# A halo row copied from the chunk above, and x loaded a chunk one step sooner, in a fused attention and deformable convolution kernel

## The chip, the cores and the metric

The kernel runs on one core of a Trainium2 chip. The metric is the device time of one launch in microseconds (us). The kernel before was timed in three runs: 5197.73 us median, from 5185.96 to 5206.68.

## The reference

The input is eight images of 256 channels and 64 x 64 positions, in float32. Two residual layers are applied:

```
x = x + L0(gn(x))
x = x + L1(gn(x))

gn: subtract the mean and divide by the deviation of each group of 8 channels over an image
L0: q, k, v = 1x1 convolutions; attention of each position over its 3x3 neighbours, 4 heads,
    plus a 3x3 kernel generated from q, k, v for every position; 1x1 projection
L1: om = conv3x3(x)                        27 channels: 9 offset pairs and 9 masks
    sample x bilinearly at 9 moved points (4 corners each), times sigmoid(mask)
    conv 3x3 of the samples, 256 -> 256 channels
```

## The kernel before

The kernel treats the images one after another. An image is cut into 8 chunks of 8 rows (512 positions); 256 channels lie as two halves of 128 partitions.

Each image has three stages. **Attention** (`attention`, L555) works through the 8 chunks, adds the result of layer 0 to the image, which stays in on-chip memory in the one tile `image`, and stores a copy of each finished chunk in DRAM. **Preparation** (`prepare`, L624) works through the 8 chunks again. In its step c it computes the sampling positions and corner weights of chunk c-1 (`positions`, L668: some 13 small VectorE instructions), writes chunk c to a table in DRAM from which the samples will be gathered (`to_table`, L630: transposes on TensorE, three ScalarE copies into the tiles `ts`, six DMAs), convolves chunk c to offsets and masks (`offsets`, L649: 18 matmuls, each recorded as two, and the ScalarE activation L665), takes the statistics of chunk c-1 of the next image (`first_stats`, L257), norms chunk c+1 of this image (`normed`, L220), and at last loads chunk c of the next image over the old chunk c (`load_chunk`, L89). **Sampling and convolution** then runs in 72 slots per image (8 chunks by 9 kernel points): in each slot four gathers by GpSimd (L771), four ScalarE scalings (L787), twelve VectorE multiply-adds (L795), eight TensorE transposes (L816), two ScalarE copies (L819) and four matmuls (L833, each recorded as two).

The slots of image b run together with the attention and the preparation of image b+1, called the front: the main loop (L876) issues one slot and then as many steps of the front as are due, 73 steps in 72 slots with a lead of six. Eight preparations are run in all. The first has no slots beside it; the last has no further image to load. The six between them do both.

The order on TensorE, ScalarE, VectorE and GpSimd is the order in which the program issues its instructions. SyncE, which issues the plain DMAs (loads of x, table writes, the chunk `r` of the kept image read back at L826, the output at L845), is ordered by a scheduler. In the built program the DMAs of one preparation stand on SyncE in this order, where xc is the load of chunk c and tc are the six table writes of chunk c: x0 t0 t1 x1 t2 x2 t3 x3 t4 x4 t5 x5 t6 x6 x7 t7. In the overlapped preparations the output DMA and the read of `r` stand inside and behind t6.

A chunk needs a row above and a row below it for the 3x3 convolution. So `normed` makes 10 rows out of `image` (9 at the first and the last chunk) into one of two tiles `xn`, of 10 rows each. For chunk c+1 it reads the last row of chunk c, and this is why the load over chunk c stands behind it. The positions of one chunk, the table transposes and the offsets of the next share a ring of four PSUM tiles (`ps_a`), so a later `offsets` can only begin when `positions` has read its tile at L689.

Of the kernel before, what the change touches and what calls it, by code (L numbers as in the profile page):

```python
# [9 lines left out]
F32 = mybir.dt.float32  # L10
I32 = mybir.dt.int32
AF = mybir.ActivationFunctionType
ALU = mybir.AluOpType
# [4 lines left out]
P = 128  # L18
C = 256
# [4 lines left out]
R = 8  # L24
N = R * W
NB = N // P
NC = H // R
# [8 lines left out]
TP = R * WP // TJ  # L36
# [21 lines left out]
def preact_kernel(ctx: ExitStack, tc: tile.TileContext, a: dict, out: bass.AP):  # L58
# [17 lines left out]
    nc = tc.nc  # L76
# [3 lines left out]
    const = ctx.enter_context(tc.tile_pool(name="const", bufs=1))  # L80
# [8 lines left out]
    def load_chunk(b, c):  # L89
        s = slice(c * N, (c + 1) * N)  # L90
        nc.sync.dma_start(image[:, :, s], sources[b][:, :, s])
# [31 lines left out]
    base = const_tile("base", [P, NC * NB, 2 * KK])  # L123
    eps = const.tile([P, 1], F32, tag="eps", name="eps")
    nc.vector.memset(eps, EPS)

    wts2 = []
    for i in range(2):
# [4 lines left out]
    xn2 = [const.tile([P, NT, R + 2, WP], F32, tag=f"xn{i}", name=f"xn{i}") for i in range(2)]  # L133
# [47 lines left out]
    p2 = ctx.enter_context(tc.tile_pool(name="p2", bufs=2))  # L181
# [6 lines left out]
    def psum_a(name):  # L188
        return ps_a.tile([P, 512], F32, tag="a", name=name)
# [27 lines left out]
            nc.vector.reciprocal(gn[:, 1, :], std)  # L217
            return gn

    def normed(xt, gn, c):  # L220

        xn = xn2[c % 2]
        lo, hi = max(0, R * c - 1), min(H, R * c + R + 1)
        if c == 0:
            nc.vector.memset(xn[:, :, 0, :], 0.0)
        if c == NC - 1:
            nc.vector.memset(xn[:, :, R + 1, :], 0.0)
        o = lo - (R * c - 1)
        for ct in range(NT):
            nc.vector.tensor_scalar(  # L230
                xn[:, ct, o : o + hi - lo, 1 : W + 1],
                xt[:, ct, lo * W : hi * W].rearrange("p (r w) -> p r w", w=W),
                gn[:, 0, ct : ct + 1],
                gn[:, 1, ct : ct + 1],
                ALU.subtract,
                ALU.mult,
            )
        return xn
# [9 lines left out]
    def window(t, ct, k):  # L248
        dy, dx = divmod(k, 3)
        if ct is None:  # L250
            return t[:, :, dy : dy + R, dx : dx + W]
        return t[:, ct, dy : dy + R, dx : dx + W]
# [4 lines left out]
    def first_stats(b, c):  # L257
        if c == 0:
            stats0[b] = p2.tile([P, NT, NC, 6], F32, tag="stats0", name=f"stats0_{b}")
        for ct in range(NT):  # L260
            nc.vector.bn_stats(
                stats0[b][:, ct, c, :], image[:, ct, c * N : (c + 1) * N]
            )
        if c == NC - 1:
            norm0[b] = Norm(stats0[b], f"0_{b}")
# [289 lines left out]
    def attention(b):  # L555
# [5 lines left out]
        yield None  # L561
        gn = gn.ready()
        xn = normed(xt, gn, 0)
        yield None
        d = None
        for c in range(NC):
# [26 lines left out]
            if c + 1 < NC:  # L593
                xn = normed(xt, gn, c + 1)
# [29 lines left out]
    def prepare(b, gn):  # L624


        xt = image
        table = tables[b % 2].rearrange("e (k c) -> e k c", k=2)

        def to_table(c, xn):  # L630
            for i in range(TJ // 2):
                ps = psum_a(f"ptab_{b}_{c}_{i}").rearrange("p (j e) -> p j e", j=2)
                for j in range(2):
                    o = WP + (2 * i + j) * TP
                    for ct in range(NT):
                        nc.tensor.transpose(
                            ps[:TP, j, ct * P : (ct + 1) * P],
                            xn[:, ct].rearrange("p r w -> p (r w)")[:, o : o + TP],
                            ident,
                        )  # L640
                ts = p2.tile([TP, 2, C], F32, tag="ts", name=f"ts_{b}_{c}_{i}", bufs=3)
                nc.scalar.copy(ts, ps[:TP])
                for q in range(2):
                    e = (R * c + 1 - q) * WP + 2 * i * TP
                    nc.sync.dma_start(
                        table[e : e + 2 * TP, q, :].rearrange("(j p) e -> p j e", p=TP), ts
                    )

        def offsets(c, xn):  # L649

            ps = psum_a(f"om_{b}_{c}")
            n = 0
            for k in range(KK):
                for ct in range(NT):
                    g = n % 4
                    nc.tensor.matmul(  # L656
                        ps[32 * g : 32 * g + 32, :],
                        w_off[:, ct, k, :],
                        window(xn, ct, k),
                        start=(n < 4),  # L660
                        stop=(n >= KK * NT - 4),
                    )
                    n += 1
            om = p1.tile([P, N], F32, tag="gs", name=f"om_{b}_{c}")
            nc.scalar.activation(om, ps, AF.Identity, bias=b_off)  # L665
            return om

        def positions(c, om):  # L668
            u = f"{b}_{c}"
            ps = psum_a(f"omt_{u}")  # L670
            for j in range(NB):
                nc.tensor.matmul(
                    ps[:, j * NOM : (j + 1) * NOM],
                    om[:, j * P : (j + 1) * P],
                    stk_om,
                    start=True,
                    stop=True,
                )
            omt = ps[:, : NB * NOM].rearrange("p (b o) -> p b o", o=NOM)
            S = [P, NB, 2 * KK]  # L680

            def small(name, shape=S, dt=F32):
                return p1.tile(shape, dt, tag=name, name=f"{name}_{u}")

            mk = small("mk", [P, NB, KK])
            nc.scalar.activation(mk, omt[:, :, 18:27], AF.Sigmoid)

            pos = small("pos")
            nc.vector.tensor_add(pos, omt[:, :, 0:18], base[:, c * NB : (c + 1) * NB, :])  # L689
            nc.vector.tensor_scalar(pos, pos, -1.0, float(H), ALU.max, ALU.min)  # L690
            pi = small("pi", dt=I32)
            nc.vector.tensor_copy(pi, pos)
            fl = small("fl")
            nc.vector.tensor_copy(fl, pi)
            gt = small("gt")
            nc.vector.tensor_tensor(gt, fl, pos, ALU.is_gt)
            nc.vector.tensor_sub(fl, fl, gt)

            fr = small("fr", [P, NB * KK, 2, 2])
            pos2 = pos.rearrange("p b (k d) -> p (b k) d", d=2)  # L700
            fl2 = fl.rearrange("p b (k d) -> p (b k) d", d=2)
            nc.vector.tensor_sub(fr[:, :, :, 1], pos2, fl2)
            nc.vector.tensor_scalar(fr[:, :, :, 0], fr[:, :, :, 1], -1.0, 1.0, ALU.mult, ALU.add)
            nc.vector.tensor_mul(
                fr[:, :, 0, :],
                fr[:, :, 0, :],
                mk.rearrange("p b k -> p (b k)").unsqueeze(2).to_broadcast([P, NB * KK, 2]),
            )
            idx = wp.tile([P, NB, KK], I32, tag="idx", name=f"idx_{u}")
            wt = wp.tile([P, NB, KK, 4], F32, tag="wt", name=f"wt_{u}")  # L710
            found[b, c] = idx, wt
            nc.vector.tensor_mul(
                wt.rearrange("p b k (x y) -> p (b k) x y", y=2),
                fr[:, :, 0, :].unsqueeze(2).to_broadcast([P, NB * KK, 2, 2]),
                fr[:, :, 1, :].unsqueeze(3).to_broadcast([P, NB * KK, 2, 2]),
            )

            fi = small("fi", [P, NB * KK])
            nc.vector.tensor_scalar(
                fi, fl2[:, :, 0], float(WP * ES), float((WP + 1) * ES), ALU.mult, ALU.add  # L720
            )
            nc.vector.scalar_tensor_tensor(
                idx.rearrange("p b k -> p (b k)"),
                fl2[:, :, 1],
                float(ES),
                fi,
                ALU.mult,
                ALU.add,
            )

        xn = normed(xt, gn, 0)
        om = None
        for c in range(NC):
            if om is not None:
                positions(c - 1, om)
            to_table(c, xn)
            om = offsets(c, xn)
            if b + 1 < B and c > 0:
                first_stats(b + 1, c - 1)
            if c + 1 < NC:  # L740
                xn = normed(xt, gn, c + 1)
            if b + 1 < B:
                load_chunk(b + 1, c)
            yield
        positions(NC - 1, om)
        if b + 1 < B:
            first_stats(b + 1, NC - 1)
        yield
# [225 lines left out]
```

## Time and profile before

| | |
|---|---|
| median of three timed runs | 5197.73 us |
| the profiled execution's own time | 5546.8 us |
| its span, first to last instruction | 5545.0 us |
| TensorE, VectorE, ScalarE, GpSimd busy | 88%, 75%, 43%, 59% of the span |
| TensorE clock granted, mean | 0.939 |
| DRAM traffic | 1280.19 MB read, 137.13 MB written |

The profiled execution is 6.7% longer than the median of the timed ones, so a sum made in its microseconds has to be carried over to the timed runs. A busy TensorE is no TensorE at its peak, since the ends of matmuls are modelled. The waits of an engine are given with the instruction that was released and with what released it.

### The profile page before, as it was taken

What the parts mean: (1) busy time and instruction counts of PE and PEld (TensorE: products, weight loads), DVE (VectorE), ACT (ScalarE), POOL (GpSimd) and SP (SyncE); (2) the same over time, 40 slices, a digit from 0 to 9 for tenths busy, and PEclk for the clock granted to TensorE, in tenths of its full rate; (3) what the DMA queues carried; (4) which work ended last, traced back from release to release, by engine and by line L of the source; (5) the groups of instructions that cost most, each with busy time, mean ns of one, the idle gap of its engine ahead of it and who ended that gap; (6) DMA issues with size and microseconds to landing.
All of it is one profiled execution on the core that took longest, in us unless ns stands there. A gap on an engine that the chain in (4) does not pass through costs nothing. (4 is left out here: it accounts for less than half of the span.)

```text
span 5545.0 us, 79699 instructions
## 1 busy us (share of the span) xinstructions
PE 4874.6 (88%) x26592; PEld 2725.8 (49%) x26592; DVE 4170.6 (75%) x10071; ACT 2368.6 (43%) x5184; POOL 3287.5 (59%) x2310
## 2 busy tenths in 40 slices
PE   7979998899988998899988999989898899887677
PEld 4545554455544554455544555445554555443333
DVE  4567787788877787778878787878777777876666
ACT  2334444444444444444444444444444444443333
POOL 0036565666646666566656666566664666647776
PEclk9989999999999999999999999999999999998878
DMA  2067777777787777877787777877778677787777
GB/s 85 21 236 251 247 249 278 262 256 260 262 311 249 266 262 283 289 247 265 260 284 278 252 268 252 302 260 258 252 256 322 242 260 258 274 300 275 274 278 279
DMA packets 476840, 1422.60 MB, mean 257 GB/s; under 512 B 46910, under 2 KB 114750, under 8 KB 476300
## 3 DMA queue, kind: packets, MB, share of 16 engines
q0 software_dynamic: 331776, 1208.11, 61.9%
q1 hardware_dynamic: 141902, 204.27, 10.2%
q10 hardware_dynamic: 2750, 5.12, 0.3%
q8 instruction: 210, 3.44, 0.2%
q14 instruction: 202, 1.65, 0.1%
HBM read 1280.19 MB, written 137.13 MB: 256 GB/s over the span
## 5 line engine op out<-in xcount | busy, mean ns | idle before, releaser
L771 POOL DMA_INDIRECT g<-table,idx x2304 | 3284.9, 1426 | 2236.2 <-DVE s L795 585.5
L795 DVE SCALAR_TENSOR_TENSOR s<-g,wt,s 128x256 f32<-128x256 f32 x6912 | 2796.0, 478 | 566.5 <-ACT s L787 399.9
L833 PE MATMUL po<-vt,w_conv 128*128 128x512 f32 x4608 | 2187.8, 620 | 63.0 <-DVE r L844 37.4
L833 PEld LDWEIGHTS po<-vt,w_conv 128*128 128x128 f32 x4608 | 880.2, 202 | 965.9 <-issue 923.9
L787 ACT ACTIVATE s<-g,wt 128x256 f32<-128x256 f32 x2304 | 1068.5, 509 | 562.5 <-DMA g<-table,idx 464.7
L816 PE MATMUL pt<-ident,s 128*128 128x128 f32 x4608 | 725.0, 295 | 262.7 <-ACT vt L819 129.9
L816 PEld LDWEIGHTS pt<-ident,s 128*128 128x128 f32 x4608 | 547.4, 149 | 557.9 <-issue 184.4
L819 ACT COPY vt<-pt 128x512 f32<-128x512 f32 x1152 | 614.7, 584 | 423.3 <-PE pt L816 271.9
L281 PE MATMUL psq<-xn,w_qkvT 128*128 128x512 f32 x512 | 291.1, 720 | 113.2 <-DVE wk L488 108.4
L359 DVE TENSOR_TENSOR qk<-qk,near_k 128x400 f32<-128x400 f32 x256 | 129.8, 567 | 306.1 <-PE qk L351 165.2
L656 PE MATMUL om<-xn,w_off 128*32 128x512 f32 x2304 | 291.9, 604 | 7.7 <-DVE pos L689 7.4
L289 ACT COPY q<-psq 128x512 f32<-128x512 f32 x128 | 75.0, 586 | 483.7 <-PE psq L281 436.2
L313 PE MATMUL psk<-xn,w_qkvT 128*128 128x264 f32 (+1 forms) x1088 | 249.3, 382 | 10.9 <-ACT k L326 10.9
L313 PE MATMUL psv<-xn,w_qkvT 128*128 128x264 f32 (+1 forms) x1088 | 258.4, 382 | 0.0
L281 PEld LDWEIGHTS psq<-xn,w_qkvT 128*128 128x128 f32 x512 | 112.1, 229 | 290.6 <-DVE wk L488 161.1
L528 ACT COPY acc<-av 128x512 f32<-128x512 f32 x128 | 74.9, 585 | 414.4 <-PE av L521 320.8
L533 PE MATMUL proj<-acc,w_projT 128*128 128x512 f32 x512 | 239.8, 596 | 3.3 <-ACT s L787 2.7
L313 PEld LDWEIGHTS psv<-xn,w_qkvT 128*128 128x128 f32 x1088 | 199.9, 190 | 83.3 <-issue 46.4
L313 PEld LDWEIGHTS psk<-xn,w_qkvT 128*128 128x128 f32 x1088 | 202.3, 191 | 73.3 <-issue 20.2
L351 PE MATMUL qk<-k,q 64*64 64x100 f32 x4096 | 165.3, 260 | 78.5 <-issue 75.4
L351 PEld LDWEIGHTS qk<-k,q 64*64 64x64 f32 x4096 | 119.4, 136 | 155.0 <-issue 139.0
L335 ACT COPY v<-psv 128x320 f32<-128x320 f32 (+1 forms) x272 | 111.5, 417 | 187.3 <-PE psv L313 171.1
(89 smaller groups left out, 3375.0 us busy)
## 6 DMA issues: line engine op xcount, KB each, us to landing
table<-ts SPq DMA_DIRECT2D x384, 176.0 KB
g<-table,idx POOLq DMA_INDIRECT x2304
x<-in_x_dram SPq DMA_DIRECT2D x64, 512.0 KB
x<-x SPq DMA_DIRECT2D x64, 512.0 KB
r<-x SPq DMA_DIRECT2D x64, 512.0 KB
out_dram<-r SPq DMA_DIRECT2D x64, 512.0 KB
w_conv<-in_w_conv_dram ACTq DMA_DIRECT2D x1, 2304.0 KB
w_qkv<-in_w_qkv_dram ACTq DMA_DIRECT2D x2, 384.0 KB
```

The source lines that it names most:

```text
L281: nc.tensor.matmul(ps, w_qkvT[:, ct, m * P : (m + 1) * P], window(self.xn, ct, 4), start=(ct == 0), stop=(ct == NT - 1),)
L313: nc.tensor.matmul(ps[:, : (hi - lo) * WP], w_qkvT[:, ct, o : o + P], self.xn[:, ct, lo:hi, :], start=(ct == 0), stop=(ct == NT - 1),)
L351: nc.tensor.matmul(both[h][64 * t : 64 * t + 64, n : n + NK], self.qt[r, ct, o * T * T : (o + 1) * T * T], kt[r, ct, :, T * o : T * o + KT ...
L359: nc.vector.tensor_mul(qk[:, 2 * jj : 2 * jj + 2, :, h, :], both[h][:, : 4 * NK].rearrange("p (j c k) -> p j c k", j=2, c=NT), near_k.unsq ...
L533: nc.tensor.matmul(ps, w_projT[:, ct, m * P : (m + 1) * P], self.acc[:, ct].rearrange("p (t y x) -> p y t x", y=T, x=T), start=(ct == 0), ...
L656: nc.tensor.matmul(ps[32 * g : 32 * g + 32, :], w_off[:, ct, k, :], window(xn, ct, k), start=(n < 4), stop=(n >= KK * NT - 4),)
L771: nc.gpsimd.indirect_dma_start(out=g, out_offset=None, in_=tables[b % 2], in_offset=bass.IndirectOffsetOnAxis(ap=found[b, c][0][:, j, k : ...
L787: nc.scalar.activation(s, g[:, 0:C], AF.Copy, scale=w[:, 0:1])
L795: nc.vector.scalar_tensor_tensor(s, g[:, q * C : (q + 1) * C], w[:, q : q + 1], s, ALU.mult, ALU.add)
L816: nc.tensor.transpose(pt[ct][:, j, :], s[:, ct * P : (ct + 1) * P], ident)
L819: nc.scalar.copy(v[:, ct, :], pt[ct].rearrange("p b n -> p (b n)"))
L833: nc.tensor.matmul(po[:, m, :], w_conv[:, ct, k, m * P : (m + 1) * P], v[:, ct, :], start=(k == 0 and ct == 0), stop=(k == KK - 1 and ct = ...
```

## The change

In the preparation, `normed` is called with `carry=True`. From the second chunk on it then no longer norms the row above the chunk again: it copies this row, for both channel halves in one instruction, from the other `xn` tile, where it was normed as the last row of the chunk above. The copy is a multiplication by a tile that holds 1.0. What `normed` makes out of `image` is 9 rows instead of 10 (8 instead of 9 at the last chunk). The attention calls `normed` as before.

With this, the norming of chunk c+1 reads only chunk c+1 and the first row of chunk c+2. So step c now loads chunk c+1 of the next image instead of chunk c, and step 0 loads chunks 0 and 1. The statistics are taken in the same steps as before. The table tiles `ts` rotate through four buffers instead of three.

On SyncE the order of a preparation becomes x0 t0 x1 t1 x2 t2 x3 t3 x4 t4 x5 t5 x6 t6 x7 t7.

```diff
+    one = const.tile([P, 1], F32, name="one")
+    nc.vector.memset(one, 1.0)
...
-    def normed(xt, gn, c):
+    def normed(xt, gn, c, carry=False):
         xn = xn2[c % 2]
         lo, hi = max(0, R * c - 1), min(H, R * c + R + 1)
+        if carry and c:
+            lo = R * c
+            nc.vector.tensor_scalar(
+                xn[:, :, 0, 1 : W + 1],
+                xn2[(c - 1) % 2][:, :, R, 1 : W + 1],
+                one,
+                None,
+                ALU.mult,
+            )
...
-                ts = p2.tile([TP, 2, C], F32, tag="ts", name=f"ts_{b}_{c}_{i}", bufs=3)
+                ts = p2.tile([TP, 2, C], F32, tag="ts", name=f"ts_{b}_{c}_{i}", bufs=4)
...
             if c + 1 < NC:
-                xn = normed(xt, gn, c + 1)
+                xn = normed(xt, gn, c + 1, carry=True)
             if b + 1 < B:
-                load_chunk(b + 1, c)
+                if c == 0:
+                    load_chunk(b + 1, 0)
+                if c + 1 < NC:
+                    load_chunk(b + 1, c + 1)
             yield
```

## The prediction

> **What bounds the kernel now.** I read the page's busy row, then the waits, then the time line of the preparations, and last the busy time by stretch.
>
> ```profile
> PE 4874.6 (88%) x26592; PEld 2725.8 (49%) x26592; DVE 4170.6 (75%) x10071; ACT 2368.6 (43%) x5184; POOL 3287.5 (59%) x2310
> ...
> DVE stats L261 <- DMA x<-in_x_dram: 72.7, 22, 9.1
> ...
> ACT ts L642 <- DMA table<-ts: 86.7, 48, 5.5
> ```
>
> TensorE has the largest share, 88%. The two waits that the change touches add up to 72.7 us on VectorE (statistics that wait for x; columns: total, times, longest) and 86.7 us on ScalarE (a copy into `ts` that waits until the tile's last table write is done). Shares don't say whether these waits count; for this I look at where they fall. In the stretch from 0 to 60 us L261 waits 7.2 us, for the first loads of the kernel, which stay. The other 65.5 us lie in the six overlapped preparations: 13.6, 10.4, 9.7, 11.9, 9.4 and 10.5 us. In each of them one wait is 8.8 to 9.1 us long, always in step 7. The time line of the second one (start, length, engine, line; in brackets the idle time before and what ended it):
>
> ```profile
> 1614.35 0.40 SPq L91 DMA_DIRECT2D x<-in_x_dram  x1
> ...
> 1631.03 1.08 SPq L91 DMA_DIRECT2D x<-in_x_dram  x2
> ...
> 1639.53 0.58 ACT L642 COPY ts<-ptab 88x512 f32<-88x512 f32 x1 [5.53 <-DMA table<-ts]
> ...
> 1643.65 1.29 DVE L261 BATCH_NORM_STATS2 stats<-x 128x6 f32<-128x512 f32 x2 [9.03 <-DMA x<-in_x_dram]
> ...
> 1647.06 1.09 PE L816 MATMUL pt<-ident,s 128*128 128x128 f32 x4 [5.23 <-DVE s L795]
> 1649.34 1.12 PE L816 MATMUL pt<-ident,s 128*128 128x128 f32 x4 [1.20 <-DVE s L795]
> ```
>
> The loads of chunks 6 and 7 are issued together at 1631.03. VectorE wants chunk 6 at 1634.6 and gets it at 1643.65. The twelve multiply-adds of the running slot stand behind the statistics in VectorE's order, and TensorE's transposes wait for their sums: 5.23 + 1.20 us idle. The other five show 6.11, 6.17, 5.97, 5.64 and 6.18 us. So VectorE's 9 us become 6 on TensorE, with 36.5 us in all six.
>
> Is TensorE what sets the pace there? Two stretches answer, from the first `positions` of a preparation to the last, the second preparation and the eighth, which loads nothing (stretch, length, busy PE, PEld, DVE, ACT, POOL, clock, DMA share, GB/s):
>
> ```profile
> 1564.53:1649.60 85.07, 78.36 (x507) 40.06 (x506) 68.47 (x198) 36.29 (x79) 37.32 (x26) 0.97 0.89 314
> 4865.25:4942.38 77.13, 77.13 (x507) 39.64 (x506) 60.92 (x184) 36.08 (x78) 26.29 (x27) 1.00 0.88 300
> ```
>
> The same 507 TensorE records take 77.13 us without a gap where nothing is loaded, and 85.07 us with 6.7 us of gaps where it is. Between the stalls a step is 11.02 us in both. TensorE sets the pace, and the stall in step 7 is on the path.
>
> **What the Trainium skill says.** "VectorE: DVE Perf Modes", section "Mode 2×_2P — use both read ports for one tensor": float32 from and to on-chip memory runs at two elements per cycle if the outermost dimension is even. The trace agrees in kind: ten rows are faster than nine.
>
> ```profile
> L230 DVE TENSOR_SCALAR xn<-x,gn 128x640 f32<-128x640 f32 x192 | 110.4, 616 | 0.0
> L230 DVE TENSOR_SCALAR xn<-x,gn 128x576 f32<-128x576 f32 x64 | 49.4, 813 | 0.0
> ```
>
> "TensorE: Matmul & The Clock Gate", section "What's actually happening": after an idle window of about 3.4 us the array runs at half clock for a while. The trace agrees: the stretch with the 5.2 us gap has clock 0.97, the one without has 1.00, and from 1646 to 1652 us it is 0.50. "DMA: Bandwidth & Descriptors", section "Queues, rings and completion order": each DMA engine takes the descriptors of one queue in ring order, so a load stands behind the table writes issued before it. This fits the 12.6 us from issue to use of chunk 6; no row here separates it.
>
> **The change part by part.**
>
> *The load a step sooner.* On SyncE chunk 6 is now issued where chunk 5 was, at 1614.35, 20 us before VectorE wants it; the slow loads of step 7 took 12 to 13 us from issue to use. The place has the same condition, the end of `normed`. Chunk 7 stays at about 1631 but alone; its statistics are wanted at 1652.7. All other loads also gain a step; chunk 0 stays, 14 us ahead. The queue between t1 and t6 is as before, each load one chunk ahead; what moves in traffic is one load of 512 KB, from step 7 to step 0. At the 301 GB/s of an early step it is 1.7 us of DMA time, where the share is 0.87 and nothing waits. Gains in the profiled execution:
> - the 36.5 us of TensorE idle in step 7;
> - smaller load waits in mid preparation (3.96 us in the first, 2.05 in the fourth) that hold `positions` and so `offsets` back: TensorE waited 2.12 + 0.64 and 0.64 + 0.84 us there, I take 3 of 4.2;
> - half clock after the gap: eight matmuls L833 took 5.08 us at 992.5 and 3.60 elsewhere. The phase is 6.8 to 10.2 us and costs at most half of that, but TensorE also waits for VectorE in it. Between 0 and 5 us each, I take 2: 12 us.
>
> Sum 51.5 us. The stretches check it: the six last 83.69, 85.07, 84.70, 86.58, 84.45 and 84.34 us against 77.13, which is 46.1 us before the clock.
>
> *The copied row.* Per image VectorE gets seven copies of 128x128 elements. No row shows one; the nearest is the 128x72 form of L690, 224 ns. Below by that, above by 128 elements at one per cycle beside it, some 0.3 us; I take 0.23. Six norms go from ten rows to nine: 2 x (813 - 616) = +0.39 us. With the copy, +0.62 us a step, six times. The seventh goes from nine rows to eight, even again: an estimate from 616 less 128 elements at two per cycle of the 0.96 GHz that the page gives (67 ns) is 0.55, so 2 x (0.55 - 0.81) + 0.23 = -0.3. In all +3.4 us per image, +27 us in eight. The rows taken out cost VectorE more than they save. What hides it: per step VectorE is busy 9.5 to 9.8 of 11.02 us and then idles 0.8 to 1.9 us before L689. Only the step with the output additions is full (13.39 busy in 13.83). If the cover were gone, `positions` would be late and, through the PSUM ring, the next `offsets` too. I let 1 us pass in each of seven preparations: -7. The first has no slots and 1.8 us of slack between norm and transposes.
>
> *Four `ts` tiles.* The wait of 5.5 us in step 7 ends before VectorE's (1639.5 against 1643.65), so today it is covered; with the load gone it would be late next, since the scalings behind it on ScalarE feed the next multiply-adds. With four tiles the third copy waits for the writes issued at 1623.1 and before, not for those up to 1626.3: some 3 us less. Worth nothing alone; it keeps the first gain.
>
> Net 51.5 - 7 = 44.5 us of 5546.8 (span and the 1.8 us around it), 0.80%. The same share of the median gives 5197.73 - 41.7 = 5156 us.
>
> **The rivals.**
> *R1, the next wait takes over.* DMA is 0.90 to 1.00 busy from 1586 to 1631 us; table writes and gathers may land late and hold ScalarE. Then half of the 36.5 us remains and no clock is saved: 18 - 7 = 11 us, 5187. For it: the 5.5 us on ScalarE. Against: step 7 loses a load, and ScalarE waits only 1.7 us for gathers in that preparation.
> *R2, the timed runs stall less than the profiled one.* They are 6.3% shorter; if loads land some 4 us sooner, the gap shrinks to 2 us, under the clock's window: 12 + 3 - 7 = 8 us, 5190.
> *R3, slower: VectorE becomes the pace.* Place: L689, before `offsets`. Price: the whole 27 us, 5223. It decides if VectorE's step with +0.62 exceeds 11.02 us and the stall was worth nothing in the timed runs. Against: 9.8 + 0.62.
> *R4, more.* VectorE is in arrears from 1644.9 to 1676 us after the stall and TensorE waits 0.5 to 1.5 us at several transposes there. If all 65.5 us of load waits and 24 us of clock count: 82.5 less, 5120.
>
> **How the numbers follow.** Likeliest case 0.60, own range 5135 to 5172; R1 0.13, R2 0.09, R3 0.08, R4 0.10. About 0.5% (26 us) is what a measurement here can tell from no change. Faster: 0.58 + 0.10 + 0.03 of R1 and R2 = 0.71. Slower: 0.06 of R3. The same: 0.23. The range 5115 to 5193 holds the likeliest, R4 and most of R1 and R2; it leaves out R3 and tails.
>
> **What would show it.** Right: L261's wait falls from 72.7 to under 15 us, and no transpose L816 waits 4 to 5 us for s at the end of a preparation; the six stretches come to 77 to 79 us; the clock there is 0.99 or more; L642 waits under 50 us; L230 has a 128x576 form at about 0.8 us as its main one. Wrong: if the stretches shorten but the attention behind them grows as much; if `offsets` waits for `positions` in most steps; or if L642's wait in step 7 stays at 5.5 us with TensorE's gap.

## The result, and the profile after

The changed kernel takes 5149.29 us (median of four runs, 5141.93 to 5153.12), the kernel before, run beside it, 5202.2 us. The ratio is 0.9897, with a 95% interval of 0.9877 to 0.9917: 53 us less, about 1%. The forecast was 5156 us and 42 us less.

One thing has to be said before two profiles are compared. The profiled execution of before that the prediction read took 5546.8 us, while the timed runs took 5197.73. The kernel before was profiled once more for the experiments (the run e0 below), and this profiled execution took 5205.18 us, as long as timed runs beside it. So the 6.7% were not the price of profiling. This second profile (span 5203.4 us, clock 0.96) is the one to set beside the profile after (span 5148.2 us, clock 0.96).

The page's busy row of the changed kernel:

```profile
PE 4726.1 (92%) x26592; PEld 2641.3 (51%) x26592; DVE 4206.1 (82%) x10128; ACT 2374.4 (46%) x5184; POOL 3193.9 (62%) x2310
```

VectorE has 57 instructions more than before: 56 row copies and one memset. It is busy 29.0 us longer than in the second profile of before (4177.1 us), in a span that is 55.2 us shorter. TensorE still has the largest share. Now the waits (total us, times, longest) of the second profile of before:

```profile
ACT ts L642 <- DMA table<-ts: 119.7, 59, 6.5
PE pt L816 <- DVE s L795: 104.3, 156, 10.3
...
DVE stats L261 <- DMA x<-in_x_dram: 83.7, 19, 9.8
```

and the same three of the changed kernel, whose lines from `normed` to `offsets` are 12 further down and whose sampling lines are 15 further down:

```profile
PE pt L831 <- DVE s L810: 73.0, 144, 10.5
...
ACT ts L654 <- DMA table<-ts: 49.0, 33, 5.5
...
DVE stats L273 <- DMA x<-in_x_dram: 12.8, 6, 3.8
```

All three fell: the statistics' wait for x by 71 us, ScalarE's wait for a `ts` tile by 71 us, and TensorE's wait for the weighted sums by 31 us. Only the last of these is on TensorE, and even that sum is not the gain, since it also holds what TensorE waits for outside the preparations. Where the time went is told by the stretches from the first `positions` of a preparation to the last. The columns are as in the prediction. First the second overlapped preparation of before, from its second profile:

```profile
1507.70:1595.00 87.30, 78.33 (x507) 40.10 (x506) 68.69 (x197) 36.46 (x79) 35.42 (x26) 0.97 0.89 315
```

then of the changed kernel the same one, and the eighth, which loads nothing:

```profile
1496.87:1574.02 77.15, 77.15 (x507) 39.64 (x506) 71.78 (x204) 35.74 (x78) 38.48 (x29) 1.00 0.95 342
4608.99:4686.13 77.14, 77.14 (x507) 39.63 (x506) 63.80 (x189) 35.30 (x78) 37.84 (x28) 1.00 0.87 304
```

TensorE is now busy without a gap, 77.15 us of 77.15, and from the second of the six on a preparation that loads is as long as one that doesn't. VectorE works 3.1 us more in it and has room for that. The six loaded preparations take 73.79, 77.15, 77.14, 77.14, 77.14 and 77.14 us, 459.5 in all. In the second profile of before they took 85.65, 87.34, 93.21, 87.33, 84.05 and 84.45, 522.0 in all. That is 62.5 us less in the preparations: TensorE's idle time in them fell from 51.4 to 0.9 us, and its busy time by 12.0 us, at a higher clock. The whole execution became 55.2 us shorter. The gain lies in the preparations, and some 7 us of it were lost elsewhere.

The time line of step 7 of that preparation in the changed kernel (start, length, engine, line; in brackets the idle time before and what ended it):

```profile
1547.20 0.39 SPq L91 DMA_DIRECT2D x<-in_x_dram  x1
...
1562.79 0.56 SPq L91 DMA_DIRECT2D x<-in_x_dram  x1
...
1564.70 0.58 ACT L654 COPY ts<-ptab 88x512 f32<-88x512 f32 x1 [0.46 <-DMA table<-ts]
...
1566.00 1.28 DVE L273 BATCH_NORM_STATS2 stats<-x 128x6 f32<-128x512 f32 x2
...
1568.36 1.09 PE L831 MATMUL pt<-ident,s 128*128 128x128 f32 x8
...
1573.54 1.07 PE L831 MATMUL pt<-ident,s 128*128 128x128 f32 x8
```

Chunk 6 is loaded at 1547.20, alone and 18.8 us before its statistics at 1566.00, which begin with no idle time before them. The transposes have none either. The `ts` copy that waited 5.53 us waits 0.46. In before, step 7 was 17.6 to 18.6 us long in the two profiles; it is 10.8 to 11.0 now.

Behind the preparation, which ends at 1574.02, TensorE does wait:

```profile
1578.89 0.38 PE L205 MATMUL gn<-mv,gmat 128*128 128x2 f32 x2 [0.85 <-DVE mv L200]
1580.90 0.74 PE L831 MATMUL pt<-ident,s 128*128 128x128 f32 x4 [1.62 <-DVE s L810]
1583.18 1.12 PE L831 MATMUL pt<-ident,s 128*128 128x128 f32 x4 [1.54 <-DVE s L810]
```

VectorE comes there with the statistics of chunk 7 and their means ahead of a slot's multiply-adds. In the 25 us behind each of the six preparations TensorE is idle for 28.6 us in all, against 15.0 in the second profile of before. So a part of the waiting has come back behind the preparation.

### The profile page after: what moved, and what is told of

It reads as the page before. It is cut to its first block, busy times and chain, and to the rows that moved or that the text cites. A ratio compares the mean times of both kernels' runs of the same rounds, so it can differ in the third digit from the quotient of the medians.

```text
span 5148.2 us, 79694 instructions
## 1 busy us (share of the span) xinstructions
PE 4726.1 (92%) x26592; PEld 2641.3 (51%) x26592; DVE 4206.1 (82%) x10128; ACT 2374.4 (46%) x5184; POOL 3193.9 (62%) x2310
## 5 line engine op out<-in xcount | busy, mean ns | idle before, releaser
L786 POOL DMA_INDIRECT g<-table,idx x2304 | 3191.4, 1385 | 1933.4 <-DVE s L810 513.4
L848 PE MATMUL po<-vt,w_conv 128*128 128x512 f32 x4608 | 2142.0, 609 | 72.5 <-DVE r L859 72.5
L848 PEld LDWEIGHTS po<-vt,w_conv 128*128 128x128 f32 x4608 | 856.6, 196 | 947.0 <-issue 866.7
L802 ACT ACTIVATE s<-g,wt 128x256 f32<-128x256 f32 x2304 | 1081.8, 509 | 545.3 <-DMA g<-table,idx 473.3
L831 PE MATMUL pt<-ident,s 128*128 128x128 f32 x4608 | 693.5, 284 | 104.9 <-DVE s L810 73.0
L831 PEld LDWEIGHTS pt<-ident,s 128*128 128x128 f32 x4608 | 519.5, 143 | 401.9 <-DVE s L810 121.3
L338 ACT COPY k<-psk 128x264 f32<-128x264 f32 (+1 forms) x272 | 100.6, 372 | 204.2 <-PE psk L325 204.0
L500 DVE TENSOR_TENSOR wk<-wk,near 100x512 f32<-100x512 f32 x256 | 158.5, 680 | 34.6 <-PE wk L492 34.6
```

The costliest lines, as they stand in the source:

```text
L500: nc.vector.tensor_mul(wk.rearrange("p (t n) -> p t n", n=T * T), ps[:NK].rearrange("p (t n) -> p t n", n=T * T), near.unsqueeze(1).to_bro ...
L786: nc.gpsimd.indirect_dma_start(out=g, out_offset=None, in_=tables[b % 2], in_offset=bass.IndirectOffsetOnAxis(ap=found[b, c][0][:, j, k : ...
L802: nc.scalar.activation(s, g[:, 0:C], AF.Copy, scale=w[:, 0:1])
L831: nc.tensor.transpose(pt[ct][:, j, :], s[:, ct * P : (ct + 1) * P], ident)
L848: nc.tensor.matmul(po[:, m, :], w_conv[:, ct, k, m * P : (m + 1) * P], v[:, ct, :], start=(k == 0 and ct == 0), stop=(k == KK - 1 and ct = ...
```

## The experiments

The theory was that of the prediction: the stall in step 7 is the late load of chunk 6, the load is late because chunk 6's last row is still to be read by the next norm, that of chunk 7, and the copied row releases it. The rivals were the four `ts` tiles (R1: the next wait takes over) and VectorE's added work (R3). The runs were made on three chips, and each ratio is against the kernel before on the same chip.

| run | what it has | ratio to before, 95% interval |
|---|---|---|
| e1 | copied row; loads at the old place in the program; 3 `ts` tiles | 0.9914 (0.9898 to 0.9931) |
| e2 | the changed kernel with 3 `ts` tiles | 0.9917 (0.9900 to 0.9933) |
| e3, e10 | before with 4 `ts` tiles, on two chips | 0.9977 (0.9966 to 0.9988), 0.9981 (0.9974 to 0.9987) |
| e7 | e1, with chunk c's last row read once more after the next norm | 1.0062 (1.0037 to 1.0086) |
| e4, e8 | before with statistics a step later; e8 with 4 `ts` tiles too | 0.9943 (0.9921 to 0.9966), 0.9936 (0.9910 to 0.9962) |
| e9 | the changed kernel, beside e4, e7 and e8 | 0.9929 (0.9904 to 0.9954) |
| e5 | the row copied for chunk 7 alone | 0.9910 (0.9894 to 0.9926) |
| e11 | e8 again, beside e5 | 0.9910 (0.9892 to 0.9927) |
| e12 | the changed kernel, beside e5 and e11 | 0.9889 (0.9871 to 0.9906) |

### Before once more

No edit: the kernel before, profiled again.

> The kernel before, unchanged, profiled a second time. Question: is the 6.7% by which its first profiled execution is longer than the timed runs a property of profiling, or of that one execution? The changed kernel's profiled execution took 5150 us, as its timed runs did. If profiling costs nothing, this one takes 5190 to 5215 us, an image's period is about 628 us instead of 660, and the six loaded preparations still take 84 to 87 us each. If profiling costs the kernel before 345 us and the changed one nothing, it takes about 5545 us again.

It took 5205.18 us, with preparations as listed above. The profile is as fast as the timed runs, and the stall is as long as in the first profile: L261's longest wait is 9.8 us against 9.1. In this one profile the stall doesn't shrink where the kernel as a whole is faster.

### The copied row alone

```diff
-                xn = normed(xt, gn, c + 1)
+                xn = normed(xt, gn, c + 1, carry=True)
             if b + 1 < B:
                 load_chunk(b + 1, c)
```

> The copied row alone: loads at their old place, three table tiles. Theory (the load is all of the gain): the stall of 9 us in step 7 stays, VectorE has some 4 us more work per image; time of before to +0.3%, 5195 to 5215 us. Rival (the norm of fewer rows frees VectorE): 0.2 to 0.5% below before, 5175 to 5190 us.

It took 5165.62 us, 0.9914 of before. The theory expected nothing of this run, and missed. SyncE's order in the built program says why: it is x0 t0 x1 t1 ... x7 t7, the same as in the changed kernel, though the line that loads stands where it stood. Once chunk c's last row isn't read by the norm of chunk c+1, the scheduler places its overwriting load a step sooner by itself. The waits of e1:

```profile
ACT ts L654 <- DMA table<-ts: 132.9, 73, 6.2
...
DVE stats L273 <- DMA x<-in_x_dram: 7.5, 4, 3.5
```

The statistics hardly wait for x; ScalarE waits more for its `ts` tiles than before (119.7 us).

### The changed kernel with three `ts` tiles

```diff
-                ts = p2.tile([TP, 2, C], F32, tag="ts", name=f"ts_{b}_{c}_{i}", bufs=4)
+                ts = p2.tile([TP, 2, C], F32, tag="ts", name=f"ts_{b}_{c}_{i}", bufs=3)
```

> The changed kernel with three table tiles: row copied, loads one chunk sooner. Theory (the load is all of the gain): ratio to before 0.989 to 0.992, 5146 to 5160 us, and ScalarE's wait for table writes in step 7 stays near 5.5 us without holding TensorE. Rival (the fourth table tile carries half of the gain, since ScalarE's wait comes next): ratio 0.994 to 0.996, about 5175 us, with a gap of 2 to 3 us before the transposes of step 7.

It took 5162.67 us, 0.9917, the same as e1: the moved `load_chunk` lines add nothing to the copied row. The preparations take 77.3, 79.4, 79.8, 80.8, 79.4 and 79.3 us, and 79.7 the one that loads nothing. The time line of step 7 in the second of them, from 1567.9 to 1579.3, shows the wait that rival R1 named:

```profile
1575.30 0.58 ACT L654 COPY ts<-ptab 88x512 f32<-88x512 f32 x1 [5.53 <-DMA table<-ts]
...
1579.03 0.83 PE L831 MATMUL pt<-ident,s 128*128 128x128 f32 x4 [0.18 <-DVE s L810]
```

With the load gone, ScalarE's 5.53 us is late next. As the theory expected, little of it reaches TensorE, whose transposes wait 0.18 us here; in the steps 7 of all six preparations TensorE is idle for 3.8 us, against 37.0 in the second profile of before. Yet the six preparations are 16.5 us longer than in the changed kernel (476.0 against 459.5), 2.75 us each; 10.1 of the 16.5 us lie in the steps 1 and 8.5 in the steps 7, and 2 are won back between. Taken from image to image 7.9 us of this remain, since TensorE waits less behind the preparations (19.9 us in the 25 us behind each, against 28.6). In whole times the fourth tile is worth 0.2% (0.9917 against 0.9897), on runs that were not made beside each other.

The preparation that loads nothing tells one thing more. With three tiles it takes 77.13 us in both profiles of before, where no row is copied, and 80.1 and 79.7 us in e1 and e2, where rows are copied; with four tiles and the copies it takes 77.14 in the profile after and in e12, and 77.40 in e9. So the copied rows cost 2.6 to 3 us of this preparation where there are three tiles, and next to nothing where there are four. Which wait brings this about was not followed.

### Four `ts` tiles alone

```diff
-                ts = p2.tile([TP, 2, C], F32, tag="ts", name=f"ts_{b}_{c}_{i}", bufs=3)
+                ts = p2.tile([TP, 2, C], F32, tag="ts", name=f"ts_{b}_{c}_{i}", bufs=4)
```

> The kernel before with four table tiles and nothing else. Theory (the load is all of the gain): same as before within 0.1%, L261 still waits 9 us in step 7. Rival (the fourth tile carries half of the gain): ratio about 0.995.

> Four table tiles and nothing else, a second time, with a second profile. If the gain of the first time (ratio 0.9977) is real, the ratio is 0.996 to 0.999 again and ScalarE's wait for table writes is again under half of what it is before; if it was the chip's drift, 0.999 to 1.001.

5194.77 us on one chip and 5193.7 on another: 0.9977 and 0.9981, both intervals below 1. The waits of the first:

```profile
DVE stats L261 <- DMA x<-in_x_dram: 83.4, 20, 9.7
ACT ts L642 <- DMA table<-ts: 45.6, 24, 5.5
```

The wait for x is untouched (83.4 against 83.7 us), ScalarE's wait falls from 119.7 to 45.6, and 9 to 10 us are gained. The theory expected no more than 0.1%, and the prediction had this part as worth nothing alone; both missed. Where the gain lies isn't shown: the six preparations are only 3.4 and 5.2 us shorter in these two profiles than in the second of before, and their steps 7 are as long as they were (106.3 and 107.2 us in all against 107.8). With e2 the two parts multiply to the whole: 0.9917 x 0.9977 = 0.9894, measured 0.9897.

### The copied row, with the old row held

```diff
                 xn = normed(xt, gn, c + 1, carry=True)
+                held = R * (c + 1) * W
+                nc.vector.tensor_scalar(
+                    held_t, xt[:, 1, held - 1 : held], one, None, ALU.mult
+                )
```

> The kernel with the copied row alone (three table tiles, loads at the old place in the program), plus one VectorE instruction of one element per step that reads the last row of chunk c behind the norm of chunk c+1. This gives the load over chunk c its old condition back; on SyncE the loads of chunks 6 and 7 again stand together before the last table writes. Theory (the copied row gains because it frees the load to start a step sooner): the wait of about 9 us in step 7 is back and the time is that of the kernel before plus the work of the copy, ratio 1.000 to 1.006. Rival (the copy itself gains, by VectorE's work or by its order): ratio 0.990 to 0.993, as without the held read.

This is e1 with a read of one element per partition, 202 ns each, that keeps chunk c's last row in use until the norm of chunk c+1 is done, as in before. The whole gain is gone, and more: 1.0062. The time line of step 7 of the second preparation:

```profile
1642.52 1.07 SPq L91 DMA_DIRECT2D x<-in_x_dram  x2
...
1655.82 1.29 DVE L274 BATCH_NORM_STATS2 stats<-x 128x6 f32<-128x512 f32 x2 [9.27 <-DMA x<-in_x_dram]
...
1659.22 1.09 PE L833 MATMUL pt<-ident,s 128*128 128x128 f32 x4 [4.64 <-DVE s L812]
1661.51 1.11 PE L833 MATMUL pt<-ident,s 128*128 128x128 f32 x4 [1.20 <-DVE s L812]
```

The loads of chunks 6 and 7 are again issued together, the statistics again wait 9.27 us, and TensorE again stands still for 4.64 + 1.20. So it is the release of the old row that brings the gain: the copying without the release brings none. The 0.6% above before, some 34 us of 5541, is not the price of the copying alone. The held read adds 11 us of VectorE work (56 times 202 ns), and SyncE's order is not quite that of before: chunk 0 is now loaded behind t0, not ahead of it, and the statistics wait for it in step 1, 24 us in the six preparations, where in before they don't wait there at all. What the copying alone costs, this run doesn't separate.

### Another way round the same stall

If the stall is the load that comes too late for its reader, the reader can be moved instead. Here the row isn't copied; the statistics of chunk c-2 are taken in step c, and those of chunks 6 and 7 both after the last step.

```diff
-            if b + 1 < B and c > 0:
-                first_stats(b + 1, c - 1)
+            if b + 1 < B and c > 1:
+                first_stats(b + 1, c - 2)
...
+            first_stats(b + 1, NC - 2)
```

> The kernel before, with no copied row and no earlier load, but the statistics of chunk c-2 instead of chunk c-1 in step c, and those of chunks 6 and 7 both behind the last step. Three table tiles. Theory (the wait for the load is the cause, whichever side is moved): the waits for x go, preparations of 78 to 81 us, ratio 0.989 to 0.993. Rival (the gain needs the load early, because late loads collide with table writes and gathers): ratio above 0.995.

> The late statistics with four table tiles: no copied row, loads at their old place. Theory: as good as the changed kernel or better by what the copied row costs VectorE where it is on the path, ratio 0.985 to 0.990. Rival (the early load has a gain of its own): 0.2% or more slower than the changed kernel.

> The changed kernel again, on the chip of the runs beside it, as their measure: ratio 0.988 to 0.991.

The last of these is the changed kernel itself. On one chip, on which before takes 5541.07 us, e4 takes 5507.88, e8 5500.44 and the changed kernel 5499.02. The wait for x falls to 7.4 us in e4, and its preparations take 74.8 to 79.5 us. All three ratios, 0.9943, 0.9936 and 0.9929, are above the ranges expected of them, so less was gained than expected; they lie within each other's intervals. So the stall can be removed without a copy on VectorE, and it is worth about as much.

### The row copied only where it counts

```diff
-                xn = normed(xt, gn, c + 1, carry=True)
+                xn = normed(xt, gn, c + 1, carry=c + 1 == NC - 1)
...
-                if c == 0:
-                    load_chunk(b + 1, 0)
-                if c + 1 < NC:
-                    load_chunk(b + 1, c + 1)
+                if c < NC - 2:
+                    load_chunk(b + 1, c)
+                if c == NC - 3:
+                    load_chunk(b + 1, NC - 2)
+                if c == NC - 2:
+                    load_chunk(b + 1, NC - 1)
```

> Row copied and load moved at the end of a preparation only: the row of chunk 7 is copied from chunk 6, step 5 loads chunks 5 and 6, step 6 chunk 7. Four table tiles. Theory A (the wait in step 7 is all that counts): as good as the changed kernel on the same chip, within 0.15%, preparations of 77 to 79 us. Theory B (the small waits for x in the first steps count too): a third of the gain is missing, 0.2 to 0.4% slower than the changed kernel, with first steps of 12 to 16 us in a part of the preparations.

> Late statistics with four table tiles, no copied row, loads at their old place, a second time, beside the changed kernel. Theory (the two are two ways of removing one wait): within 0.15% of the changed kernel on this chip. If the copied row's work on VectorE (38 us in all) costs time, this is 0.2% or more faster than the changed kernel.

> The changed kernel beside the three others on one chip: ratio 0.989 to 0.994, depending on the chip (0.9897 and 0.9929 so far).

The last of these is again the changed kernel. e5 copies one row per image instead of seven and has the load of chunk 6 alone a step sooner; that of chunk 7 keeps its place on SyncE, though its line moved. These three ran on one chip: 5152.4 us for e5, 5154.82 for the late statistics with four tiles, 5144.39 for the changed kernel. The changed kernel is ahead by 0.16 and 0.2%, just outside the 0.15% expected. The intervals of the ratios overlap, but all five runs of the changed kernel (5139.41 to 5147.93) lie below all six of e5 (5148.59 to 5161.61) and below five of the six of e11 (5145.71 to 5166.18), so on this chip the lead is probably real. In e5 the statistics wait 35.3 us for x in all, four times for 3 to 6 us in step 2, and the first four preparations take 78 to 79.5 us, 8.8 us more in all six than in e12: moving every load, not only that of chunk 6, seems to be worth a little. The preparations of e11 are about as long as in the changed kernel (460.3 us in six against 461.0); its images take 624 to 626 us against 621 to 623, so its rest lies behind the preparation. The profiled execution of e11 was the longest of its six, so this difference is rather too large. Two statistics instead of one stand there ahead of the next stage, but that this is the cause was not tested. Nothing that was run beats the changed kernel.

## Why the prediction was right, and where its sum was off

**The bound and the stall.** Right. TensorE set the pace, the wait of 9 us in step 7 was on its path, and without it a preparation runs at the pace of one that loads nothing: 77.14 to 77.15 us, where the prediction said 77 to 79 (73.79 in the first, which has less TensorE work in it: 73.28 us busy in the first profile of before, where the others have 77.6 to 78.4). e7 shows that the gain goes when the load is held back again.

**SyncE's order as the mechanism.** Right in what it does, but not in what brings it about: the prediction put it down to the moved load, and e1 shows that the moved lines are idle. What counts is the last reader of the old row.

**36.5 + 3 + 12 us for the stall, small waits and half clock.** The stretches fell by 49.3 us against the profile that the prediction used: 43.7 us of TensorE's idle time, where 39.5 had been reckoned, and 5.6 us of its busy time. Against the second profile of before, whose third preparation alone was 93.21 us, they fell by 62.5 us: 50.5 idle and 12.0 busy. The clock in the stretch shown went from 0.97 to 1.00 as foreseen from the Trainium skill ("TensorE: Matmul & The Clock Gate", section "What's actually happening"), since the idle window is gone. But the part of the term that was reckoned for the half clock behind the stretch did not come as a gain. In the second profile of before the clock goes to half some 3.5 to 5.7 us before each of the six preparations ends; in the changed kernel it goes to half 6 to 9 us behind the end, for 3.4 to 10.2 us, near the waits shown above. In the 25 us behind the six preparations the half clock lasts 32.0 us in all before and 41.0 after. From image to image before and after differ by 58.8 us in all, nearly 4 us less than the stretches alone.

**The copied row.** VectorE's busy time rose by 29.0 us where 27 had been reckoned, and by 3.1 in the stretch. The groups by shape (us in all, mean ns of one) show the parts:

```profile
L242 DVE TENSOR_SCALAR xn<-x,gn 128x576 f32<-128x576 f32 x144 | 116.3, 849 | 0.0
...
L242 DVE TENSOR_SCALAR xn<-x,gn 128x640 f32<-128x640 f32 x96 | 55.2, 616 | 0.0
...
L229 DVE TENSOR_SCALAR xn<-xn,one 128x128 f32<-128x128 f32 x56 | 19.1, 342 | 0.3
...
L242 DVE TENSOR_SCALAR xn<-x,gn 128x512 f32<-128x512 f32 x16 | 6.9, 474 | 0.0
```

The copy takes 342 ns on average (280 in the median), not 0.23 us and on average above the upper bound of 0.3; the nine-row form takes 849, not 813; the eight-row form 474, not 550. The sum of these rows less the two of before is 38 us. The busy time rose by less, mostly because the records of neighbouring groups overlap (7 us of these rows), so that the hit on 27 us owes something to luck. That nine rows cost more than ten decided the sign of this term. The Trainium skill ("VectorE: DVE Perf Modes", section "Mode 2×_2P — use both read ports for one tensor") asks for an outermost dimension that is even, or odd and equal in source and destination. The trace records the norm's source as one run of elements (640, 576 or 512 in a partition) and its destination as ten, nine or eight rows of 64: with nine rows the two are neither both even nor equal. The run agrees with that: 616, 849 and 474 ns. What passes on to the path was put at 7 us. With 77.14 us in the stretches it is nothing in the preparations, but only with four tiles, as the eighth preparation of e1 and e2 shows.

**"Worth nothing alone" for the four tiles.** This sub-step failed. It is worth 0.2% alone (e3 and e10), 9 to 10 us, and as much on top of the rest. The reasoning, that the 5.5 us are covered by VectorE's longer wait, holds for step 7, which e3 and e10 leave as long as it was; that nothing else could gain from the tile was put down without a reason, and what does gain was not found. "It keeps the first gain" is right in kind: with three tiles the preparations are 2.75 us longer each, and 7.9 us of that remain from image to image. ScalarE's wait, forecast under 50 us, is 49.0 in the profile after and 52.0 and 53.5 in e9 and e12.

**The scaling by share.** Also wrong. It rests on a profiled execution of 5546.8 us being 6.7% longer than the timed ones for all its parts alike. The second profile shows the preparations no shorter in an execution of 5205 us, so the saving should have been carried over in us: 5197.73 - 44.5 = 5153. That leaves some 9 us to the 53 measured, which no single term accounts for. The sum had 51.5 us less 7 for the copied row. The preparations gave back 49.3 or 62.5 us, by the profile of before that is taken, the copied row took nothing from them, and some 7 us of the 62.5 were lost outside, which the sum did not have. That the total came so near is in part luck.

**The rivals.** R1's size was seen in e2, without the fourth tile: 2.75 us per preparation where half of the stall would be 3, but the larger part of it in step 1, and the run takes 5162.67 us, not R1's 5187. R2 lost its premise with the second profile: the longest wait was 9.8 us in an execution as fast as the timed ones. R3 needs `offsets` to wait for `positions`; TensorE's wait of that kind, 11.6 us in all in the second profile of before, is at most 0.9 us in the three profiles of the changed kernel. R4's 5120 us would need 82.5 us, and the preparations gave back at most 62.5.

## What to carry to other kernels

When an in-place load is late, look for the last reader of the old data rather than for the line that loads: copying one row away from it let the scheduler move the load by itself, and moving the line did nothing more. Moving the reader instead (e4, e8) brought about as much. Follow a wait onto the engine that sets the pace before pricing it, and compare the stretch with one of the same kind that lacks the suspected cause; here that gave 46 us beside the 49 to 62 found. Look behind the stretch as well, for part of a wait can come back there. Carry a stall from one execution to another in microseconds, not in per cent, unless it is shown to scale.

## What was not expected of the hardware

The same program takes 5203.69 and 5203.87 us on two of the chips and 5541.07 us on a third, 6.5% more. The profiles taken on the third show a granted clock of 0.937 to 0.941, the others 0.960 to 0.967. The first profile of before, at 0.939 and 5546.8 us, looks like one of the third kind, which is inferred and not recorded. Its preparations were no longer than on the others (508.8 us in six against 522.0); the difference lies between them, in images of 655 to 664 us against 628 to 639, and its cause stays open. On that chip the change saves 39 us of 5541 (25 to 53 by its interval); the two other comparisons gave 53 and 58, and whether that is a real difference isn't settled.

On VectorE a norm of ten rows takes 616 ns, of nine 849 and of eight 474, and a copy of a quarter of the eight rows' elements still takes 342: the smaller piece is not cheaper in proportion, so cutting rows off an instruction can cost more than it saves.
